# The head of a macaron block, written out in one order: setup, seven norms and five first FFNs

## The chip, the core and the metric

The kernel runs on one core of a Trainium2 chip. The metric is the device time of one execution in microseconds. Three runs of the kernel before took 2293.59, 2293.7 and 2294.9 us; their median is 2293.7.

A core has five engines that run side by side, each through its own list of instructions in order: TensorE (PE in the profile) multiplies matrices into PSUM, VectorE (DVE), ScalarE (ACT) and GpSimd (POOL) do elementwise work, and SyncE (SP) issues most of the transfers. An instruction that waits holds back all that stand behind it on its engine.

## The reference

The input is (4, 4096, 512) in float32, 128 row tiles of 128 rows. One block of a macaron transformer is computed:

```python
x = x + 0.5 * ffn(layernorm(x))
x = x + attention(layernorm(x))
x = x + 0.5 * ffn(layernorm(x))
```

`ffn` rounds its input and its 512x512 weight to a 6-bit grid in blocks of 32 (a scale from the largest magnitude of each block, then the nearest point of the grid), multiplies, and adds a bias; both calls share weight and bias. `attention` is neighbourhood attention with 16 heads of 32, in which each position sees 13 neighbours, with a table of relative position biases, a projection to Q, K and V and one out.

## The kernel before

**Data.** Each float32 operand of a product is split into two float16 parts, high and low. A product is three passes over four chunks, 12 matmuls of 128x128 by 128x512 (`product`, L139). The weights lie transposed and split in `wt`. A row tile's split operand is transposed by a DMA that SP issues (`low`, L195: DVE makes the low part, SP transposes both).

**One tile's way.** Load (`load`, L167), statistics, then the quantised norm (`quantised_norms`, L213): POOL makes the factors, ACT the normed tile `yq`, DVE the blocks' scales, POOL divides by them, ACT rounds to 8 bits, POOL scales back, ACT writes the high part of `hlq`, DVE the low, SP transposes into `xT`. Then the first FFN (`first_half`, L274): PE multiplies, DVE adds to x, statistics, POOL's factors, ACT, DVE, and a transpose into `x2`. Then V (`values`, L296). For each of the 128 items (a group of four tiles by a quarter of the heads) come Q and K (`project_qk`, L354: two products, ACT's high parts `qf` and `qk`, DVE's low parts, two spreading copies on ACT), scores (`ps`), softmax, attention (`attend`), the projection out, the last norm, the second FFN and the store.

**The order of the work.** The loop is a software pipeline written as slots: `begin(slot, stage, rank)` puts a stage into a slot, `run_slot` runs the stages of one slot by rank, and a stage is a generator whose `yield n, rank` puts its rest n slots further on. An item takes STEP = 7 slots. The first Q and K product stands in slot QK = 38.

**The head.** Everything ahead of slot 38 is the head (L673 to L891). Its first part, the setup, is left to a scheduler that orders instructions itself. It loads the FFN's weight `fw`, three biases on ACT's queue, three tiles of x and 16 chunks of the other weights (`rows`); takes the sums of squares of every weight chunk (ACT, 20 of them), from which `powers` makes the powers of two that put each weight on a good scale for float16; rounds the FFN's weight to the grid and scales it back with its power of two in `w_back` (L776, L780); splits it (L782, L783) and transposes it; and makes the norms of tiles 0 to 2. From L793 on the order is the program's own: the slots up to 37 run tiles 3 to 6 up to their norms, the first FFN of tiles 0 to 4, V of tiles 0 to 2, `put_scaled` (L795: ACT's high part and DVE's low part of one weight chunk, then its transpose) for the 16 chunks in slots 2 to 35, the attention bias `pmb` (L834, a product of its own) and the table of position biases (`put_table`).

**Buffers.** PSUM has three buffers for products (`ps_m`). The norms ahead of the loop share one `hlq`, one `q8` and two `yq`; split weights have four buffers (`whl`); `xT` has three. `qk`, `qf` and the loop's other tiles lie in memory that the setup's pools give back at L894.

Of the kernel before, what the change touches and what calls it, by code (L numbers as in the profile page):

```python
# [26 lines left out]
F32 = mybir.dt.float32  # L27
# [10 lines left out]
P = 128  # L38
HEADS = 16
# [24 lines left out]
def macaron_kernel(  # L64
# [148 lines left out]
    def quantised_norms(slot):  # L213
# [7 lines left out]
        if spare:  # L221
            y = xp.tile([P, dim], F32, tag="x", name=f"yq{slot}").unsqueeze(1)
        else:
            y = yp.tile([P, 2, dim], F32, tag="yq", bufs=2, name=f"yq{slot}")[:, :n]
# [16 lines left out]
        q8 = q8p.tile([P, 2, dim], F8, tag="q8", name=f"q8_{slot}")[:, :n]  # L241
# [6 lines left out]
        if spare:  # L248
            hl = xp.tile([P, dim], F32, tag="x", name=f"hlq{slot}").bitcast(F16)
            hl = hl.rearrange("p (u s k) -> p u s k", u=1, s=2)  # L250
        else:
            hl = hlp.tile([P, 2, 2, dim], F16, tag="hlq", name=f"hlq{slot}")[:, :n]
# [351 lines left out]
    EARLY = 3  # L604
# [35 lines left out]

    for t in range(NT):
        k = t * STEP
        sooner = (0, 2, 5, STEP)[t] if t <= EARLY else 0
        begin(k - 18 - (STEP if t == EARLY else 0), one(load, t), 0)
        slot = k - 10 - (10 if t == EARLY else 0)
        enlist(slot, t, "n1")
        if not 0 < t < EARLY:
            begin(slot - 1, one(moments, slot, t, "n1"), 1)
        begin(k + F1 - sooner, first_half(t))
        begin(k + V, values(t))  # L650
        begin(k + F1 - sooner, one(add_bias, t, half_ffn_b), 8)
# [6 lines left out]
    for slot in together:  # L658
        if together[slot][0][0][1] == "n3" or together[slot][0][0][0] >= EARLY:
            begin(slot, quantised_norms(slot), 1)  # L660
# [11 lines left out]

    with tc.tile_pool(name="setup", bufs=1) as sp, tc.tile_pool(name="scratch", bufs=2) as scr:  # L673
# [4 lines left out]
        rp = sp.tile([HEADS, NREL + 2 * (QR - 1)], F32, name="rp")  # L678
        for o in range(KC):
            nc.sync.dma_start(out=fw[:, o, :], in_=ffn_w[o * P : (o + 1) * P, :])  # L680
        nc.scalar.dma_start(out=half_ffn_b, in_=ffn_b.partition_broadcast(P))
        nc.scalar.dma_start(out=after_b, in_=proj_b.partition_broadcast(P))
        nc.scalar.dma_start(out=b12, in_=qkv_b.rearrange("(c p) -> c p", p=P))
        nc.gpsimd.memset(rp, 0.0)
        nc.scalar.dma_start(out=rp[:, QR - 1 : QR - 1 + NREL], in_=rpb)


        rows = {}

        sq = sp.tile([P, 5 * KC], F32, name="sq")  # L690
        first = min(slots)
        for slot in range(first, first + EARLY * STEP, STEP):
            run_slot(slot)
        for _ in quantised_norms(-10):
            pass
        chunks = (8, 9, 10, 11, 12, 13, 14, 15, 0, 4, 1, 5, 2, 6, 3, 7)
        for o in chunks:
            w, i = (qkv_w, o) if o < 3 * KC else (proj_w, o - 3 * KC)
            rows[o] = xp.tile([P, dim], F32, tag="x", name=f"rows{o}")
            nc.sync.dma_start(out=rows[o], in_=w[i * P : (i + 1) * P, :])  # L700
        for o in (*range(4 * KC, 5 * KC), *chunks):
            src = fw[:, o - 4 * KC, :] if o >= 4 * KC else rows[o]
            junk = scr.tile([P, dim], BF16, tag="junk", name=f"junk{o}")
            nc.scalar.activation(junk, src, AF.Square, accum_out=sq[:, o : o + 1])
        ptb = ps_m.tile([P, 512], F32, tag="mm", name="ptb")
        nc.tensor.transpose(ptb[:, : 3 * KC], b12, ident[: 3 * KC, : 3 * KC])
        bT = sp.tile([P, 3 * KC], F32, name="bT")
        nc.vector.tensor_copy(bT, ptb[:, : 3 * KC])
        b2 = sp.tile([P, 3 * KC], F32, name="b2")
        nc.vector.scalar_tensor_tensor(b2, bT, 2.0 ** -8, bT, ALU.mult, ALU.mult)  # L710
        nc.vector.tensor_tensor(sq[:, : 3 * KC], sq[:, : 3 * KC], b2, ALU.add)
        top5 = sp.tile([P, 5], F32, name="top5")
        up = sp.tile([P, 5], F32, name="up")
        down = sp.tile([P, 5], F32, name="down")

        def powers(lo, hi):

            w = hi - lo
            nc.vector.tensor_reduce(
                top5[:, lo:hi], sq[:, lo * KC : hi * KC].rearrange("p (m c) -> p m c", c=KC),  # L720
                AX.X, ALU.max,
            )
            ptn = ps_m.tile([P, 512], F32, tag="mm", name=f"ptn{lo}")
            nc.tensor.transpose(ptn[:w, :P], top5[:, lo:hi], ident)
            most = sp.tile([w, 1], F32, name=f"most{lo}")
            nc.vector.tensor_reduce(most, ptn[:w, :P], AX.X, ALU.max)
            diag = sp.tile([w, w], F32, name=f"diag{lo}")
            nc.vector.tensor_scalar(diag, ident[:w, :w], most, 2.0, ALU.mult, ALU.mult)
            ones_w = sp.tile([w, P], F32, name=f"ones{lo}")
            nc.gpsimd.memset(ones_w, 1.0)  # L730
            pb = ps_m.tile([P, 512], F32, tag="mm", name=f"pb{lo}")
            nc.tensor.matmul(pb[:, :w], ones_w, diag, start=True, stop=True)
            e = sp.tile([P, w], I32, name=f"e{lo}")
            nc.vector.tensor_copy(e.bitcast(F32), pb[:, :w])
            nc.vector.tensor_scalar(e, e, 23, None, ALU.logical_shift_right)
            nc.vector.tensor_scalar(e, e, 131, None, ALU.add)
            nc.vector.tensor_scalar(e, e, 1, None, ALU.logical_shift_right)
            nc.vector.tensor_scalar(e, e, 97, None, ALU.max)
            u, d = up[:, lo:hi].bitcast(I32), down[:, lo:hi].bitcast(I32)
            nc.vector.tensor_scalar(u, e, -1, 264, ALU.mult, ALU.add)  # L740
            nc.vector.tensor_scalar(u, u, 23, None, ALU.logical_shift_left)
            nc.vector.tensor_scalar(d, e, -10, None, ALU.add)
            nc.vector.tensor_scalar(d, d, 23, None, ALU.logical_shift_left)

        powers(4, 5)
        nc.vector.tensor_scalar(cf, down[:, 4:5], 0.5 / XS, None, ALU.mult)
        nc.gpsimd.tensor_scalar(half_ffn_b, half_ffn_b, 0.5, None, ALU.mult)

        def put_weights(o, hl):
            return nc.sync.dma_start_transpose(  # L750
                out=wt.rearrange("p s c o -> p (s c) o")[:, :, o * P : (o + 1) * P],
                in_=hl.rearrange("p s k -> p (s k)"),
            )

        w_sc, w_r, w_back = (
            sp.tile([P, KC * NB], F32, name=name) for name in ("w_sc", "w_r", "w_back")
        )
        for o in range(KC):  # L760
            nc.vector.tensor_reduce(
                w_sc[:, o * NB : (o + 1) * NB], blocks(fw[:, o, :]), AX.X, ALU.max,
                apply_absolute_value=True,
            )
        nc.vector.tensor_scalar(
            w_sc, w_sc, F8_SCALE / Q_MAX, F8_SCALE * Q_EPS, ALU.mult, ALU.max
        )
        nc.vector.reciprocal(w_r, w_sc)

        def per(t, o):  # L770
            return bc(t[:, o * NB : (o + 1) * NB], QB)

        for o in range(KC):
            fwb = blocks(fw[:, o, :])
            nc.vector.tensor_tensor(fwb, fwb, per(w_r, o), ALU.mult)
        nc.vector.tensor_scalar(w_back, w_sc, up[:, 4:5], None, ALU.mult)  # L776
        for o in range(KC):
            w8 = scr.tile([P, dim], F8, tag="w8_", bufs=KC, name=f"w8_{o}")
            nc.scalar.activation(w8, fw[:, o, :], AF.Identity, bias=w_nudge, saturate=False)
            nc.vector.tensor_tensor(blocks(fw[:, o, :]), blocks(w8), per(w_back, o), ALU.mult)  # L780
            hl = scr.tile([P, 2, dim], F16, tag="whl", bufs=4, name=f"whlf{o}")
            nc.scalar.copy(hl[:, 0, :], fw[:, o, :])  # L782
            nc.vector.tensor_tensor(hl[:, 1, :], fw[:, o, :], hl[:, 0, :], ALU.subtract)  # L783
            put_weights(4 * KC + o, hl)

        for t in range(1, EARLY):
            moments(t * STEP - 10, t, "n1")
            for _ in quantised_norms(t * STEP - 10):
                pass

        ctx.enter_context(tc.manual_schedule())  # L793

        def put_scaled(o):  # L795
# [6 lines left out]
            )  # L802
            put_weights(o, hl)

        su, sd = up, down
        tab = sp.tile([P, 1], F32, name="tab")
        vb = sp.tile([P, KC], F32, name="vb")

# [129 lines left out]
```

## Time and profile before

| | us |
|---|---|
| median of three runs | 2293.7 |
| the profiled execution, its own time | 2295.28 |
| its span, from first to last instruction | 2293.5 |
| first quantised tile's product pmf on PE | 37.04 |
| first Q and K product pmqk on PE | 82.39 |
| Q and K product of item 1 | 98.07 |
| Q and K product of item 2 | 109.21 |

Busy us of the engines, from the profile by stretch:

| stretch, us | PE | DVE | ACT | POOL | DMA share |
|---|---|---|---|---|---|
| 0 to 100 | 47.55 | 68.72 | 58.85 | 47.83 | 0.72 |
| 100 to 200 | 99.49 | 97.01 | 88.27 | 83.49 | 0.76 |
| 300 to 400 | 100.00 | 90.47 | 76.25 | 89.08 | 0.73 |
| 2000 to 2100 | 100.00 | 89.03 | 77.48 | 88.76 | 0.71 |
| 2100 to 2200 | 89.86 | 78.97 | 70.82 | 78.37 | 0.66 |

A row of the timeline gives the start, the time on the engine, the engine (SPq is SP's queue: the time that issuing takes), the line, the operation, what is written and from what, the count, and in brackets the idle time before it and what ended that. The chain of waits is the sequence of work that ended last, followed back from the last instruction. PE's granted clock is 1.00 at full speed.

### The profile page before, as it was taken

What the parts mean: (1) busy time and instruction counts of PE and PEld (TensorE: products, weight loads), DVE (VectorE), ACT (ScalarE), POOL (GpSimd) and SP (SyncE); (2) the same over time, 40 slices, a digit from 0 to 9 for tenths busy, and PEclk for the clock granted to TensorE, in tenths of its full rate; (3) what the DMA queues carried; (4) which work ended last, traced back from release to release, by engine and by line L of the source; (5) the groups of instructions that cost most, each with busy time, mean ns of one, the idle gap of its engine ahead of it and who ended that gap; (6) DMA issues with size and microseconds to landing.
All of it is one profiled execution on the core that took longest, in us unless ns stands there. A gap on an engine that the chain in (4) does not pass through costs nothing.

```text
span 2293.5 us, 65425 instructions
## 1 busy us (share of the span) xinstructions
PE 2214.2 (97%) x26771; PEld 1052.9 (46%) x26771; DVE 2011.7 (88%) x3769; ACT 1695.5 (74%) x2544; POOL 1969.2 (86%) x2006
## 2 busy tenths in 40 slices
PE   3799999999999999999999999999999999999978
PEld 1344444444444444444444444444444444444433
DVE  6899998888988988898988998888988988989775
ACT  5697777777777777777777777777777777777752
POOL 4588988988988988888888888888888889888776
PEclk9999999999999999999999999999999999999989
DMA  7687776777767777777776776777776777866654
GB/s 201 153 178 161 162 160 154 159 162 158 160 156 155 164 162 154 161 158 157 162 158 155 162 161 154 160 157 155 164 160 151 167 158 154 166 155 147 137 107 104
DMA packets 926213, 359.61 MB, mean 157 GB/s; under 512 B 719452, under 2 KB 890328, under 8 KB 925912
## 3 DMA queue, kind: packets, MB, share of 16 engines
q1 hardware_dynamic: 925568, 354.90, 70.8%
q8 instruction: 209, 3.42, 0.6%
q14 instruction: 92, 0.75, 0.1%
q10 hardware_dynamic: 344, 0.53, 0.1%
HBM read 110.26 MB, written 67.29 MB: 77 GB/s over the span
## 4 chain that ended last, share of the span: by engine, by line
PE 87%; DVE 7%; ACT 2%; POOL 2%; DMA 1%; issue 1%; SPq 0%; ACTq 0%; DVEq 0%; POOLq 0%
PE pmqk L144 27%; PE pmf L144 26%; PE pmo L144 14%; PE pmv L144 13%; PE ps L458 4%; PE pv L549 3%; DVE stn L173 1%; DVE hlq L197 1%; DVE hln L197 1%; DVE sc L232 1%; ACT qk L390 0%; DVE x L272 0%; POOL yq L239 0%; DVE total L514 0%; DVE qf L383 0%
## 5 line engine op out<-in xcount | busy, mean ns | idle before, releaser
L144 PE MATMUL pmf<-wt,xT 128*128 128x512 f16 x3048 | 702.7, 381 | 13.3 <-DMA xT<-hlq 7.4
L144 PE MATMUL pmqk<-x,wt 128*128 128x512 f16 x3072 | 705.8, 379 | 0.4 <-DVE after_b L836 0.4
L144 PEld LDWEIGHTS <-xT 128*128 128x128 f16 x3048 | 298.4, 98 | 377.2 <-DMA xT<-hlq 15.2
L144 PEld LDWEIGHTS <-wt 128*128 128x128 f16 x3072 | 289.7, 98 | 336.0 <-issue 1.3
L239 POOL TENSOR_TENSOR yq<-yq,r 128x1024 f32<-128x1024 f32 (+1 forms) x141 | 247.1, 1752 | 135.6 <-DVE r L237 124.1
L144 PE MATMUL pmv<-wt,x 128*128 128x512 f16 x1536 | 353.9, 380 | 4.2 <-DVE qf L383 2.6
L144 PE MATMUL pmo<-wt,ring 128*128 128x512 f16 x1536 | 357.2, 383 | 0.0
L390 ACT ACTIVATE qk<-qf,parity 128x1024 f16<-128x1024 f16 x256 | 349.3, 1432 | 0.0
L610 POOL TENSOR_TENSOR x<-x,half_ffn_b 128x512 f32<-128x512 f32 x256 | 327.8, 1281 | 0.0
L272 DVE SCALAR_TENSOR_TENSOR x<-pmf,coef,x 128x512 f32<-128x512 f32 x256 | 180.0, 703 | 144.7 <-PE pmf L144 141.1
L576 ACT ACTIVATE ring<-pv 128x510 f16<-128x510 f32 (+7 forms) x176 | 78.7, 475 | 307.3 <-PE pv L549 234.4
L173 DVE BATCH_NORM_STATS2 stn<-x 128x6 f32<-128x512 f32 x384 | 265.2, 691 | 8.8 <-DMA x<-in_L_attn_x_dram 0.2
L244 POOL TENSOR_TENSOR yq<-q,sc 128x1024 f32<-128x1024 fp8e4 (+1 forms) x141 | 246.2, 1746 | 4.8 <-ACT q L242 4.8
L144 PEld LDWEIGHTS <-x 128*128 128x128 f16 x1536 | 150.5, 98 | 186.9 <-issue 4.9
L242 ACT ACTIVATE q<-yq,nudge 128x1024 fp8e4<-128x1024 f32 (+1 forms) x141 | 150.0, 1064 | 115.9 <-POOL yq L239 107.6
L144 PEld LDWEIGHTS <-ring 128*128 128x128 f16 x1536 | 141.2, 98 | 160.5 <-issue 5.0
L518 POOL TENSOR_TENSOR sf<-sf,total 128x714 f32<-128x714 f32 (+2 forms) x128 | 178.7, 1396 | 37.2 <-DVE total L516 19.3
L226 ACT ACTIVATE yq<-x,nbq,rsq 128x512 f32<-128x512 f32 x254 | 193.1, 803 | 16.7 <-POOL nbq L185 15.2
L525 POOL TENSOR_TENSOR p<-sf,p 128x714 f16<-128x714 f32 (+2 forms) x128 | 192.5, 1504 | 0.0
L509 POOL TENSOR_TENSOR sf<-sf,top 128x714 f32<-128x714 f32 (+2 forms) x128 | 182.4, 1425 | 3.5 <-DVE top L507 3.3
L197 DVE TENSOR_TENSOR hlq<-yq,hlq 128x1024 f16<-128x1024 f32 (+1 forms) x141 | 167.6, 1189 | 8.7 <-ACT hlq L193 6.6
L610 POOL TENSOR_TENSOR x<-x,after_b 128x512 f32<-128x512 f32 x128 | 162.9, 1274 | 0.0
(143 smaller groups left out, 3441.0 us busy)
## 6 DMA issues: line engine op xcount, KB each, us to landing
vs<-vd SPq DMA_DIRECT2D x144, 357.0 KB
x<-in_L_attn_x_dram SPq DMA_DIRECT2D x128, 256.0 KB
vd<-vt SPq DMA_DIRECT2D x128, 256.0 KB
out_dram<-x SPq DMA_DIRECT2D x128, 256.0 KB
vs<-vd SPq DMA_DIRECT2D x24, 378.0 KB
vs<-vd SPq DMA_DIRECT2D x24, 315.0 KB
rows<-in_L_attn_qkv_w_dram SPq DMA_DIRECT2D x12, 256.0 KB
xT<-hlq SPq DMA_TRANSPOSE x141
```

The source lines that it names most:

```text
L144: nc.tensor.matmul(pm, lhs(a, c), rhs(b, c), start=(n == 0), stop=(n == 3 * KC - 1))
L173: nc.vector.bn_stats(st, xs[t])
L197: nc.vector.tensor_tensor(hl[:, :, 1, :], y, hl[:, :, 0, :], ALU.subtract)
L226: nc.scalar.activation(y[:, u], xs[t], AF.Identity, bias=nb[:, u : u + 1], scale=rs[:, u : u + 1])
L239: nc.gpsimd.tensor_tensor(yb, yb, bc(r, QB), ALU.mult)
L244: nc.gpsimd.tensor_tensor(yb, q8.rearrange("p u (n q) -> p (u n) q", q=QB), bc(sc, QB), ALU.mult)
L272: nc.vector.scalar_tensor_tensor(xs[t], pm, cf, xs[t], ALU.mult, ALU.add)
L390: nc.scalar.activation(to, whole[0], AF.Copy, scale=parity[:, e : e + 1])
L509: nc.gpsimd.tensor_tensor(s, s, bc(top[:, :n], KN), ALU.subtract)
L518: nc.gpsimd.tensor_tensor(s, s, bc(total[:, :n], KN), ALU.mult)
L525: nc.gpsimd.tensor_tensor(p[:, :n, KN : 2 * KN], s, ph, ALU.subtract)
L610: nc.gpsimd.tensor_tensor(xs[t], xs[t], b, ALU.add)
```

## The change

The whole head becomes one list of pieces, each with a number, and is issued by the program in the order of these numbers (`at`, `spread_out`, L878 to L964 of the changed kernel); nothing of it is left to the scheduler, and no slot below 38 is used. The numbers run from 0.7 to 69.0; they set the order and nothing else. In detail:

- The list holds the setup, the norms of tiles 0 to 6 to their end, the first FFN of tiles 0 to 4 to its end and V of tiles 0 and 1. V of tile 2 goes into slot 39, and the product `pmb` of the attention bias into slot 47, behind item 1's Q and K product.
- The seven norms get buffers of their own for `yq`, `q8` and `hlq`, one tile each, in the setup's pool. `xT` still has three buffers.
- The FFN's weight is scaled back without its power of two (`per(w_sc, o)`, `w_back` is gone); the power is applied when it is split, by the same `split` that splits the other chunks.
- The biases `half_ffn_b` and `after_b` and the table `rpb` are loaded on SP's queue behind 27 loads; only the QKV bias is left on ACT's.
- The other 16 weight chunks are split after the first FFN of tile 1, four buffers as before.
- Two dozens of matmuls whose result nobody reads stand on PE behind the first and the last split of the FFN's weight.

```diff
-    def quantised_norms(slot):
+    def quantised_norms(slot, own=None):
...
-        if spare:
+        if own:
+            y = own.tile([P, 1, dim], F32, name=f"yq{slot}")
+        elif spare:
...
-        nc.vector.tensor_scalar(w_back, w_sc, up[:, 4:5], None, ALU.mult)
...
-            nc.vector.tensor_tensor(blocks(fw[:, o, :]), blocks(w8), per(w_back, o), ALU.mult)
-            hl = scr.tile([P, 2, dim], F16, tag="whl", bufs=4, name=f"whlf{o}")
-            nc.scalar.copy(hl[:, 0, :], fw[:, o, :])
-            nc.vector.tensor_tensor(hl[:, 1, :], fw[:, o, :], hl[:, 0, :], ALU.subtract)
...
+        def scaled_back(o):
+            nc.vector.tensor_tensor(blocks(fw[:, o, :]), blocks(w8[o]), per(w_sc, o), ALU.mult)
+
+        def split(o):
+            s = up[:, o // KC : o // KC + 1]
+            hl = scr.tile([P, 2, dim], F16, tag="whl", bufs=4, name=f"whl{o}")
+            nc.scalar.activation(hl[:, 0, :], rows[o], AF.Copy, scale=s)
+            yield
+            nc.vector.scalar_tensor_tensor(
+                hl[:, 1, :], rows[o], s, hl[:, 0, :], ALU.mult, ALU.subtract
+            )
+            nc.sync.dma_start_transpose(
...
+            if o in (4 * KC, 5 * KC - 1):
+                idle = ps_s.tile([P, 512], F32, tag="s", name=f"idle{o}")
+                for _ in range(12):
+                    nc.tensor.matmul(idle, hl[:, 1, :P], hl[:, 1, :], start=True, stop=True)
...
-        begin(0, one(scales), 9)
-        for slot, o in zip((2, 4, 5, 6, 10, 13, 16, 19, 21, 23, 25, 27, 29, 31, 33, 35), chunks):
-            begin(slot, put_scaled(o), 9)
-        begin(20, attention_bias(), 9)
-        begin(26, one(put_table), 9)
...
+        for o, key in enumerate((0.7, 1.1, 1.6, 2.0)):
+            at(key, load_ffn, o)
+        for t, key in enumerate((2.4, 2.9, 5.0, 5.4, 7.6, 11.4, 11.9, 57.0, 64.0)):
+            at(key, load, t)
...
+        at(12.3, lambda: nc.sync.dma_start(out=half_ffn_b, in_=ffn_b.partition_broadcast(P)))
+        at(12.7, lambda: nc.sync.dma_start(out=after_b, in_=proj_b.partition_broadcast(P)))
+        at(13.2, lambda: nc.sync.dma_start(out=rp[:, QR - 1 : QR - 1 + NREL], in_=rpb))
+        at(14.9, lambda: nc.gpsimd.tensor_scalar(half_ffn_b, half_ffn_b, 0.5, None, ALU.mult))
+        for h in range(4):
+            at(13.6 + 0.5 * h, put_masks, h)
+        at(15.8, put_shifts)
+        for i, key in enumerate((16.6, 17.2, 24.3, 24.9, 25.5, 26.1, 26.7, 27.3)):
+            at(key, put_shifted, i // 4 * 2, i % 4)
...
+        for o, h, l in zip(
+            (8, 9, 10, 11, 0, 4, 1, 5, 2, 6, 3, 7, 12, 13, 14, 15),
+            (40.2, 40.9, 41.6, 42.3, 43.1, 44.4, 45.9, 46.7, 48.8, 49.5, 50.3, 51.0, 54.6, 55.3, 56.6, 57.4),
+            (41.9, 42.6, 44.1, 45.7, 46.5, 47.2, 51.0, 51.7, 52.5, 53.2, 53.9, 56.0, 58.6, 60.1, 61.7, 62.5),
+        ):
+            spread_out(split(o), h, l)
...
+        NORMS = (
+            (6.3, 7.3, 9.1, 11.7, 12.9, 15.9, 17.4, 18.9, 20.1),
+            (14.9, 16.2, 20.2, 21.5, 22.8, 24.3, 25.1, 26.7, 27.4),
+            (22.7, 23.9, 25.8, 28.1, 29.9, 31.4, 33.5, 35.0, 36.7),
...
+            (26.5, 42.7, 51.7, 63.9, 65.1, 66.3, 67.1, 68.3, 69.0),
+        )
+        for t, keys in enumerate(NORMS):
+            slot = t - 1000
+            enlist(slot, t, "n1")
+            at(keys[0], moments, slot, t, "n1")
+            spread_out(quantised_norms(slot, sp), *keys[1:])
+        FIRST = (
+            (26.0, 29.3, 31.2, 32.3, 33.6, 35.1),
+            (31.2, 33.9, 35.8, 36.8, 38.1, 40.5),
...
+        for t, (keys, bias) in enumerate(zip(FIRST, (15.0, 21.1, 27.4, 31.0, 40.2))):
+            spread_out(first_half(t), *keys)
+            at(bias, add_bias, t, half_ffn_b)
...
+        for _, _, f, args in sorted(order, key=lambda e: e[:2]):
+            f(*args)
...
+    begin(QK + 1, values(2), 6)
+    begin(QK + 9, bias_product(), 9)
+    slot = QK
```

## The prediction

> **What bounds the kernel now.** I read the page first: PE is busy 97% of the span, and the row of 40 slices puts nearly all that is missing into the first two slices. Then busy time by stretch, cut where item 1's Q and K product starts (98.07, from the PE timeline) and at 2100.
>
> ```profile
> PE 2214.2 (97%) x26771; PEld 1052.9 (46%) x26771; DVE 2011.7 (88%) x3769; ACT 1695.5 (74%) x2544; POOL 1969.2 (86%) x2006
> ```
> ```profile
> 98.07:2100.00 2001.93, 1999.98 (x24557) 955.90 (x24550) 1804.82 (x3349) 1533.63 (x2276) 1778.18 (x1766) 1.00 0.73 159
> ```
> From 98.07 to 2100 PE is idle for 1.95 us (column two less column three). Whatever the head saves or loses moves everything behind it by as much. So the question is when item 1's pmqk starts in the changed kernel, and which PE work stands ahead of it. The PE timeline around it:
>
> ```profile
> 82.39 5.50 PE L144 MATMUL pmqk<-x,wt 128*128 128x512 f16 x24 [0.43 <-DVE after_b L836]
> 87.73 2.75 PE L144 MATMUL pmf<-wt,xT 128*128 128x512 f16 x12
> 93.10 4.21 PE L144 MATMUL pmv<-wt,x 128*128 128x512 f16 x12 [2.62 <-DVE qf L383]
> 97.24 0.90 PE L458 MATMUL ps<-qk 64*64 64x84 f16 x64
> 98.07 5.35 PE L144 MATMUL pmqk<-x,wt 128*128 128x512 f16 x24
> ```
> Last comes the chain of waits. It ends the head on ACT's first qf (91.58), held by a weight transpose: the qf tile lies in memory that the setup gives back. Two more views price the changed head: SP's issues, and what the DMA engines moved in each us from 0 to 40.
>
> ```profile
> 88.34 3.05 DMA wt<-whl
> 91.58 0.69 ACT qf L379
> ```
> ```profile
> 24.50 4.11 SPq L750 DMA_TRANSPOSE wt<-whlf  x3
> ...
> 31.44 2.71 SPq L847 DMA_DIRECT2D shifted<-rd  x4
> ...
> 78.19 2.69 SPq L750 DMA_TRANSPOSE wt<-whl  x2
> ```
> ```profile
> GB/s 0 53 154 195 227 384 400 380 291 293 264 313 387 391 408 408 397 391 391 387 385 358 143 3 0 45 204 192 180 182 254 134 142 51 32 160 128 53 37 104
> ```
> So SP needs 1.35 us for a transpose and 0.65 for a shifted copy, and the loads run at about 390 GB/s, 0.67 us for each 256 KB.
>
> **What ends the changed head.** In the changed kernel's order of instructions qf of item 0 waits for the transpose of norm 6, the last DMA of the head; its own tiles lie where qf goes. I call the landing of that transpose Tq (91.58 in before) and the start of item 1's pmqk T1 (98.07). The PE work ahead of T1 is as before, less pmb, whose 12 matmuls (2.6 us) now come behind it. So the change costs T1 - 98.07 + 2.6.
>
> **Step 1, the loads.** In the code a DMA on SP waits until the eighth before it has landed. Before, x0 stood still till 5.78 for half_ffn_b, and its 26 loads (6.8 MB) were in at about 22.4. Now half_ffn_b is the 28th load: two more are 1.3 us, and the dip in slices 8 to 11 (0.4 MB short of 390, 1.0 us) may fill. I take 22.5; the ends are 20.5 (28 at 0.67 from 1.7) and 23.7. The written order wants it at 14.9, and POOL, which runs in order, has the half of it (1.51) and x0's bias (1.27) ahead of norm 1's factors (three small ones, 1.2 with gaps) and of norm 0's scaling back (1.1): done at 27.6. ACT's high part (0.62) and DVE's low part (0.68) follow: 29.0. Before, that low part began at 26.21.
>
> **Step 2, the first two FFNs.** SP stands at rd until rp has landed, just behind the biases (23.0), then issues rd (0.69), one weight transpose (25.1), waits for rd (unseen; as a transpose's 2.8 us, 26.4), two shifted copies (27.7), two weights (30.4), norm 0 (31.7), the last FFN weight, which lands at 31.7 + 2.8 = 34.5. pmf_0 begins there, 2.5 us ahead of before (37.04). Six shifted copies (3.9) stand ahead of norm 1's transpose: issued 37.0, landed 39.8, pmf_1 done at 42.5. Its x (0.72), three DVE pieces ahead in the queue (0.28, 0.22 and a low part at 0.6 from start to start), statistics (0.85), factors (1.4, as from 59.23 to 60.64), yn and its high part (1.33) and the low part (0.69) end at 48.6.
>
> **Step 3, SP from there.** Behind it SP has 24 transposes (16 of them weights) and 4 copies (0.55 each): 24 x 1.35 + 2.2 = 34.6 us. Never waiting, the last is issued at 48.6 + 34.6 - 1.35 = 81.9 and lands at 84.7. It will wait. The 16 weights share four buffers; from the fifth on, ACT's split (0.72) needs a landed transpose, so a chunk takes (0.72 + 0.75 + 1.35 + landing) / 4: 1.41 at 2.8 us, 1.7 if landing grows to 4 in a full queue (a load already took 5: issued 7.89, used 12.84). That is up to 4.2 over twelve chunks. Norm 6 ends in a chain of POOL, ACT, POOL, ACT, DVE (1.05, 0.72, 1.04, 0.61, 0.68 = 4.1) that two transposes (2.7) don't cover: up to 1.4. So Tq is 84.7 to 90.3; no row is nearer to either end, and I take the middle, 87.5. With the loads at their ends it would be 85.5 or 88.7.
>
> **Step 4, from Tq to T1.** Three PSUM buffers are held by pmqk's two and pmv_2, so pmf_5 waits for qf's low part: 0.69 + 0.75. In before it had run ahead (87.73). PE has then stood for some 8 us. After 2.62 us of standing pmv took 4.21 instead of 2.75, after 4.54 pmf took 4.45, after 1.54 pmv took 2.76. So: 1.5 + 4.45 + pmv 2.6 + ps 0.83 = 9.4, against 6.5 in before. T1 = 96.9.
>
> **Sum.** 96.9 - 98.07 + 2.6 = +1.4. The profiled execution took 2295.28 (span 2293.5), 1.6 above the median of the three runs; against the median the forecast is 2293.7 + 1.4 = **2295.1**.
>
> **Edits at nothing.** Own hlq buffers take away ACT's two waits for a landed transpose (1.35 and 1.71), but POOL's late half_ffn_b is now what hlq waits for. The power of two at the split takes away w_back (0.82) and lengthens four copies by 0.11 and four DVE low parts by about 0.1: nothing, as DVE stands before low part 0 anyway. The 24 idle matmuls (0.44 each cold, 10.6) lie where PE stood 22.9 us; they cost only if the second dozen, from about 29.7, runs past 34.5 (5.3 cold: by 0.5). The masks stand at POOL's start in the trace of before too (2.03 to 3.66). Seven norms done ahead shorten no part of the loop: there PE sets the pace, and after_b's 0.75 on DVE falls under a DVE of 90%.
>
> Of the idle dozens the Trainium skill says, in "TensorE: Matmul & The Clock Gate", section "What's actually happening", that the array falls to half rate after an idle window of about 3.4 us. The trace shows it slow after 2.62 already. By the rule or by the row the dozens may keep pmf_0 warm (2.75 for 5.30), which is 2.5 us on x0, but pmf_1 waits for norm 1's transpose (39.8) either way, and pmf_5 is cold: the sum is the same.
>
> **Rivals.**
> *Faster: the written order nearly holds.* half_ffn_b lands by 18 (it isn't issued before the 20th load is in, 1.7 + 20 x 0.67 = 15.1, and takes a lone transpose's 2.8), and SP then starts its run five to seven us earlier, until DVE is the limit: from x0's update to the end its queue is 35 us of work. For it: the dip of slices 8 to 11 and the slow first five us may both go. Against it: loads came at the full rate, with 5 us from issue to use. Tq = 80, T1 = 89.4, 2287.6. Chance 0.17.
> *Slower: the four weight buffers set the pace.* ACT runs in order; while a split waits for a landed transpose, yn and the high parts of the first FFNs stand behind it, and SP behind those, which delays the landing of the next. It decides once issue to landing passes 2.6 us (1.35 x 4 less 0.72, 0.75 and 1.35), and the rows have 2.8 to 3.05 with an unloaded queue. At 4.4 a chunk takes 1.8, twelve of them 5.4 over SP's pace, on top of 87.5: Tq = 92.9, T1 = 102.3, 2300.5; POOL and DVE in each other's way (whl's low part 0.88 in the mean, 0.74 at its shortest, sixteen times) makes it 2302.7. Against it: before has this loop too, and there DVE, not ACT, was late for most chunks (2.3 us of waiting for ACT's split in sixteen). Chance 0.33.
> *About the same: SP sets the pace, as summed.* Own range 2289 to 2299. Chance 0.50.
>
> **The numbers.** The range reaches half way into both rivals: 2286.5 to 2303. A difference of 0.2%, 4.6 us, is about what a measurement here tells from none. Faster 0.17, within it 0.50, slower 0.33.
>
> **What would show it.** Right: half_ffn_b's half on POOL at 21 to 24; pmf_0 near 34.5; SP's transposes back to back from about 48; qf waiting for norm 6's transpose at about 87.5; pmf_5 at 4.2 us or more. Wrong: half_ffn_b by 18, or ACT rather than SP waiting longest between 48 and 85, or a loop in which PE stands for more than 2 us between T1 and 2100.

## The result and the profile after

The changed kernel takes **2305.28 us** (median of five runs, 2304.0 to 2306.06) against 2293.7 of the kernel before in the same comparison (2293.19 to 2295.01): ratio 1.0050, 95% interval 1.0038 to 1.0061, 11.6 us slower. Its profiled execution took 2305.28 (span 2303.3), 10.0 more than that of before. The forecast was 2295.1, the range ended at 2303.

The shares in the page's busy row are as they were within one per cent, since PE sets the pace of the whole (its 24 further matmuls are the idle ones). The stretch behind the start of item 1's pmqk (T1, now 107.18), from the view by stretch (columns as before), is as full as it was too:

```profile
PE 2223.0 (97%) x26795; PEld 1054.9 (46%) x26795; DVE 2015.3 (87%) x3770; ACT 1695.9 (74%) x2544; POOL 1968.4 (85%) x2006
```
```profile
107.18:2100.00 1992.82, 1990.85 (x24450) 950.56 (x24443) 1796.08 (x3330) 1522.71 (x2263) 1767.95 (x1755) 1.00 0.74 159
```
From T1 to 2100 PE is idle for 1.97 us (1992.82 less 1990.85; 1.95 before). So the loss lies in the head. PE's timeline of it:

```profile
36.92 2.75 PE L144 MATMUL pmf<-wt,xT-1000_358 128*128 128x512 f16 x12 [1.33 <-issue]
41.88 4.45 PE L144 MATMUL pmf<-wt,xT-999_453 128*128 128x512 f16 x12 [2.21 <-DMA xT-999_453<-hlq-999_448]
...
82.17 7.48 PE L144 MATMUL pmqk<-x,wt 128*128 128x512 f16 x24 [8.77 <-DVE r-995_772 L239]
...
98.95 5.04 PE L144 MATMUL pmf<-wt,xT-995_804 128*128 128x512 f16 x12 [6.70 <-DVE qf L390]
...
107.18 1.04 PE L144 MATMUL pmqk<-x,wt 128*128 128x512 f16 x4
```
The first tile's FFN begins where it did (36.92; 37.04 before), item 0's pmqk too (82.17; 82.39), and T1 is 9.1 us later. The chain of waits of the head tells what was late:

```profile
18.29 4.79 DMA after_b<-in_L_attn_proj_b_dram
23.13 1.51 POOL half_ffn_b L901
...
39.08 2.76 DMA xT-999_453<-hlq-999_448
...
57.42 3.27 DMA wt<-whl
...
61.57 3.22 DMA wt<-whl
...
71.39 3.23 DMA wt<-whl
...
80.70 3.09 DMA wt<-whl
...
94.27 3.04 DMA xT-994_828<-hlq-994_826
```
The names: xT-1000 to xT-994 are the transposed norms 0 to 6. The chain passes through the late biases, through norm 1's transpose, four times through the landing of a weight transpose, and ends on norm 6's. ACT's waits, up to 110 us (total, times, longest):

```profile
ACT whl L808 <- DMA wt<-whl: 15.4, 6, 5.7
ACT hlq-1000_352 L193 <- POOL yq-1000_249 L249: 8.8, 1, 8.8
...
ACT qf L386 <- DMA xT-994_828<-hlq-994_826: 4.3, 1, 4.3
```
Line one is ACT standing at a split until a weight buffer is free again; line two is norm 0 behind the late half_ffn_b; line three is qf, which the prediction let wait for norm 6. In the kernel before no split waited so: its 16 other weights begin at 42.62 and take 47 us, here they begin at 57.42 and go through the same four buffers in 31.

### The profile page after: what moved, and what is told of

It reads as the page before. It is cut to its first block, busy times and chain, and to the rows that moved or that the text cites. A ratio compares the mean times of both kernels' runs of the same rounds, so it can differ in the third digit from the quotient of the medians.

```text
span 2303.3 us, 65461 instructions
## 1 busy us (share of the span) xinstructions
PE 2223.0 (97%) x26795; PEld 1054.9 (46%) x26795; DVE 2015.3 (87%) x3770; ACT 1695.9 (74%) x2544; POOL 1968.4 (85%) x2006
## 4 chain that ended last, share of the span: by engine, by line
PE 89%; DVE 5%; DMA 2%; ACT 2%; POOL 1%; issue 1%; SPq 0%; ACTq 0%; POOLq 0%; DVEq 0%
PE pmqk L144 27%; PE pmf L144 27%; PE pmo L144 14%; PE pmv L144 13%; PE ps L465 4%; PE pv L556 3%; DVE stn L173 1%; DMA wt<-whl 1%; DVE hlq L197 0%; DVE hln L197 0%; ACT qk L397 0%; DVE sc L234 0%; POOL yq L241 0%; POOL yq L249 0%; DVE x L279 0%
## 5 line engine op out<-in xcount | busy, mean ns | idle before, releaser
L144 PE MATMUL pmf<-wt,xT 128*128 128x512 f16 x2988 | 686.4, 380 | 6.9 <-DMA xT<-hlq 5.5
L144 PEld LDWEIGHTS <-xT 128*128 128x128 f16 x2988 | 291.7, 98 | 361.9 <-DMA xT<-hlq 7.7
L241 POOL TENSOR_TENSOR yq<-yq,r 128x1024 f32<-128x1024 f32 (+1 forms) x136 | 241.3, 1774 | 121.1 <-DVE r L239 108.3
L249 POOL TENSOR_TENSOR yq<-q,sc 128x1024 f32<-128x1024 fp8e4 (+1 forms) x136 | 240.9, 1772 | 1.9 <-ACT q L247 1.9
```

The lines of the kernel that those rows point to most:

```text
L144: nc.tensor.matmul(pm, lhs(a, c), rhs(b, c), start=(n == 0), stop=(n == 3 * KC - 1))
L241: nc.gpsimd.tensor_tensor(yb, yb, bc(r, QB), ALU.mult)
L249: nc.gpsimd.tensor_tensor(yb, q8.rearrange("p u (n q) -> p (u n) q", q=QB), bc(sc, QB), ALU.mult)
```

## The experiments

**Theory A:** two costs one behind the other, POOL's 8.2 us of waiting for half_ffn_b and, later, the four weight buffers. **Rivals:** the late bias alone (B), SP's 1.35 us a transpose (C), POOL's chain of the last norms (D). The first three runs also test whether the parts add up; a fourth takes up the order in which memory comes free. T1 below is that of the profiled execution; "against before" is the median less that of before in the same comparison.

| run | T1 | against before, us | ratio, 95% |
|---|---|---|---|
| after | 107.18 | +11.6 | 1.0038 to 1.0061 |
| e1, bias first | 108.62 | +14.7 | 1.0047 to 1.0077 |
| e2, six weight buffers | 103.52 | +8.7 | 1.0022 to 1.0050 |
| e3, e1 and e2 | 105.19 | +12.2 | 1.0034 to 1.0064 |
| e5, norms 5 and 6 in the loop's tiles | 101.97 | +7.5 | 1.0020 to 1.0043 |
| e6, copies late | 108.82 | +14.4 | 1.0047 to 1.0074 |
| e7, e1 and e6 | 106.89 | +11.8 | 1.0035 to 1.0062 |
| e8, e2, e5 and e7 | 98.08 | +4.4 | 1.0010 to 1.0028 |
| e9, no pmb | 107.16 | +10.7 | 1.0027 to 1.0055 |
| e10, e1 and the copies in SP's gap | 102.87 | +7.3 | 1.0020 to 1.0044 |
| e11, e2, e5 and e10 | 94.72 | -0.5 | 0.9990 to 1.0008 |
| e12, e11 and pmb in the head | 95.56 | -2.0 | 0.9983 to 1.0001 |
| e13, before with the power at the split | 97.00 | -0.9 | 0.9987 to 1.0005 |
| e15, e2 and e5 | 98.68 | +4.9 | 1.0011 to 1.0030 |
| e4, no idle matmuls | 107.02 | +10.1 | 1.0029 to 1.0062 |

### The bias, the buffers, the release of memory

e1:
```diff
-        at(12.3, lambda: nc.sync.dma_start(out=half_ffn_b, ...
+        at(0.8, lambda: nc.scalar.dma_start(out=half_ffn_b, ...
```


> Edit: half_ffn_b is loaded on ACT's queue beside b12, at the very start, in place of the 28th load on SP's; nothing else. T1 is the start of item 1's Q and K product (107.18 after, 98.07 before), and behind it nothing should change, so the time should follow T1 one for one. Theory A (two costs: POOL stands 8.2 us for half_ffn_b at about 23, and later the four weight buffers set the pace): the half runs before 12 us, norm 0's low part ends near 22 in place of 28.95, the run of weight transposes begins 3 to 6 us sooner, and the buffers still hold it: T1 102 to 104, 2300 to 2302. Rival B (the late bias is the whole loss): T1 at or under 98, 2295 or less. Rival C (the four buffers, or SP, set the pace from 48 on whatever comes before): T1 within 1.5 of 107.2, 2304 to 2306.

Norm 0's low part came 4.5 us sooner (24.44 for 28.95), and nothing followed: PE stood 9.2 us for a weight transpose, and pmf_0 began later than in the kernel after.

```profile
38.09 5.01 PE L144 MATMUL pmf<-wt,xT-1000_358 128*128 128x512 f16 x12 [9.23 <-DMA wt<-whl]
```
T1 is 108.62. B falls, and so does that half of A: a wait of eight us on three engines gave nothing back when it was taken away. The edit has prices of its own, though. SP's loads waited 2.2 us for half_ffn_b, rd left 0.67 us later (24.71), and pmf_0 ran slower (5.01 for 2.75; below, "cold" and "warm"). What lay beside the wait is in SP's timeline of the kernel after:

```profile
24.04 0.65 SPq L850 DMA_DIRECT2D rd<-rp  x1
...
28.24 1.27 SPq L854 DMA_DIRECT2D shifted<-rd  x2
29.61 2.65 SPq L813 DMA_TRANSPOSE wt<-whl  x2
...
35.04 3.93 SPq L854 DMA_DIRECT2D shifted<-rd  x6
39.08 1.26 SPq L198 DMA_TRANSPOSE xT-999_453<-hlq-999_448  x1
```
rd waits for the last load, the first shifted copy waits for rd to land (28.24), the FFN's weights stand behind it, and six more copies stand ahead of norm 1's transpose, whose low part began at 36.00 and took 0.69.

e2:
```diff
-            hl = scr.tile([P, 2, dim], F16, tag="whl", bufs=4, name=f"whl{o}")
+            hl = scr.tile([P, 2, dim], F16, tag="whl", bufs=6, name=f"whl{o}")
```


> Edit: six buffers for the split weights in place of four; nothing else. ACT waits 15.4 us for landed weight transposes in the kernel after. Theory A (the buffers set the pace): these waits fall under 4 us, norm 6's transpose is issued 5 to 9 us sooner (94.27 after), T1 98 to 102, 2296 to 2300. Rival C (SP's 1.35 us a transpose sets the pace, and ACT's waits are only its image): ACT's waits shrink but T1 moves by less than 1.5, 2304 to 2306. Rival D (POOL's chain of the last norms sets it): the weights end sooner, but norm 6's transpose is issued within 2 us of 94.27, T1 105 or later, 2303 or more.

```profile
ACT whl L808 <- DMA wt<-whl: 8.2, 7, 3.3
```
```profile
90.23 1.24 SPq L198 DMA_TRANSPOSE xT-994_828<-hlq-994_826  x1
```
ACT's waits for landed weights fell from 15.4 to 8.2, norm 6's transpose was issued at 90.23 (94.27), T1 103.52. The gain is under the forecast of A, but T1 moved by 3.7 where C allowed 1.5, so C falls; and D, which had norm 6 hardly moved, falls too. The buffers are a real part of the loss, though A had made too much of them.

> Edit: both of the above, half_ffn_b at the start on ACT's queue and six weight buffers. Theory A: the two add up, as they act on two stretches one behind the other: T1 94 to 98, 2291 to 2296. If they are one cost seen twice: T1 no lower than the better of the two alone, by 1.5. With SP as the pace behind 48 (rival C): T1 as in the kernel with the bias first alone.

The two edits together: T1 105.19, worse than the buffers alone by about what the bias edit costs alone (1.7 and 1.4). That is also the sign that was set for one cost seen twice, but a cost seen twice would have shown a gain in e1 too. So the early part of A was wrong and the late part stands.

e5:
```diff
-            spread_out(quantised_norms(slot, sp), *keys[1:])
+            spread_out(quantised_norms(slot, sp if t < 5 else None), *keys[1:])
```


> Edit: the last two of the seven norms take the loop's tiles in place of own ones in the setup's pool; nothing else. Then the setup's memory is free without norm 6's transpose having landed, and qf of item 0 should wait for the table's last operation (92.93 to 93.6) in place of the landing at 97.31. Theory A (a part of the loss sits in the order of release, apart from pace and bias): qf near 93.6, pmf_5 some 3.7 us sooner, T1 103 to 104, 2301 to 2302. Rival (norm 6's high part now waits for norm 5's landed transpose and eats the gain): T1 106 to 108, 2304 to 2306.

As expected by A, and more: ACT's timeline has qf at 93.91, behind DVE's last operation on the setup's tiles, no longer behind a transfer.

```profile
93.91 0.69 ACT L386 ACTIVATE qf<-pmqk,qk_b 128x512 f16<-128x512 f32 x1 [0.54 <-DVE vbx L876]
```
pmf_5 then began at 95.92 (98.95) and ran warm, 2.75 for 5.04, so T1 is 101.97: 5.2 us, of which 2.3 is PE's clock. That part can't be counted on: in e11 the same product stood as long (3.06 us; 3.08 here) and ran cold, 4.40. qf needs nothing of norm 6. It waited only because norm 6's own tile lay in the pool whose memory qf's pool takes over.

### The copies in SP's order

**Theory E:** SP's order holds the first FFNs (rd, the copies), and POOL's late bias counts only once that is mended. e6 moves the nine issues; e7 is e6 with e1.
```diff
-        at(15.8, put_shifts)
-        for i, key in enumerate((16.6, 17.2, 24.3, 24.9, 25.5, 26.1, 26.7, 27.3)):
+        at(36.0, put_shifts)
+        for i, key in enumerate((36.8, 36.9, 37.0, 37.1, 37.2, 37.3, 37.4, 37.5)):
```


> Edit: the copy rd<-rp and the eight copies shifted<-rd are issued on SP behind norm 2's transpose and ahead of norm 3's, in place of among the FFN's weights and ahead of norm 1's transpose; nothing else. New theory E (what the run with the bias first taught: POOL's 8.2 us wait was cover, not cost; SP's order holds the first two FFNs, as rd waits there for rp, the first shifted copy for rd, and six more stand ahead of norm 1's transpose): norm 1's transpose follows its low part (36.0 to 36.7) in place of 39.08, pmf_1 begins near 39.6 (41.88), and all behind it moves up as much: T1 104 to 105.5 (107.18), 2302 to 2303.5. With half_ffn_b still late, no more than 3 us can come. Rival F (the late bias and SP each cover the other, so neither alone gives anything): T1 within 1 of 107.2, 2304.5 to 2306.

> Edit: the copies late as in the run beside this one, and half_ffn_b first on ACT's queue; nothing else. Theory E: with both gone pmf_0 begins at 30 to 33 (36.92) and pmf_1 at 35 to 37 (41.88): T1 100 to 102.5, 2298 to 2301. So the bias, which alone gave nothing (T1 108.62), would be worth some 3 us more once SP is out of the way. Rival F': the loads themselves (FFN weights, then x) or DVE's queue hold pmf_1 at 39 or later: T1 no lower than with the copies late alone.

Half right. pmf_1 began at 39.78 in e6 (expected 39.6) and at 36.93 in e7 (35 to 37), from 41.88. But T1 was 108.82 and 106.89: the gain was given back at once. SP in e7:

```profile
50.26 5.15 SPq L854 DMA_DIRECT2D shifted<-rd  x8
...
56.88 1.25 SPq L198 DMA_TRANSPOSE xT-997_600<-hlq-997_578  x1
58.23 2.67 SPq L813 DMA_TRANSPOSE wt<-whl  x2
```
Norm 3's low part began at 51.31, its transpose was issued 4.9 us behind the low part's end, and the first of the other weights (58.23; 57.42 in the kernel after) behind that. The copies cost what they delay, wherever they stand. In e7 SP stood from 33.4 (xT-999's issue) to 44.86; e10 puts them there, right behind norm 1's transpose, with the bias first:
```diff
-        at(15.8, put_shifts)
-        for i, key in enumerate((16.6, 17.2, 24.3, 24.9, 25.5, 26.1, 26.7, 27.3)):
+        at(27.6, put_shifts)
+        for i, key in enumerate((28.0, 28.2, 28.4, 28.6, 28.8, 29.0, 29.2, 29.4)):
```


> Edit: half_ffn_b first on ACT's queue, and rd with the eight shifted copies issued on SP right behind norm 1's transpose (SP stood there from 33.4 to 46.9 in the run with the copies late and the bias first); nothing else. Theory E, place by place: the nine issues cost what they delay. Among the FFN's weights they held pmf_0 and pmf_1, ahead of norm 3's transpose they held that and the first weight (56.88 and 58.23, with the low part ready at 51.3). In the gap they should delay nothing: norm 3's transpose near 52.7, first weight transpose 53.5 to 55, T1 102 to 104 (106.89), 2299.5 to 2302. Rival: the gap is no gap, as rd's wait or the copies' queue holds norm 2's transpose past 48: T1 106 or later, 2304 or more.

```profile
33.30 0.65 SPq L850 DMA_DIRECT2D rd<-rp  x1
37.31 5.16 SPq L854 DMA_DIRECT2D shifted<-rd  x8
...
52.73 1.26 SPq L198 DMA_TRANSPOSE xT-997_600<-hlq-997_578  x1
54.08 6.80 SPq L813 DMA_TRANSPOSE wt<-whl  x5
```
It all came as written: norm 3's transpose 52.73, first weight 54.08, T1 102.87, +7.3 us, 2301.2. SP's 3.3 us of waiting for rd are still there, and now they hold nobody. The pair of edits is worth 4.3 us of T1. No run has the copies there with the bias still late, so how the 4.3 divides is not shown.

### Both stretches, pmb, and the parts costed at nothing

> Edit: copies late, bias first, six weight buffers, the last two norms in the loop's tiles; the other parts of the change stay. Theory E with A: the gains act one behind the other (first FFNs 5 to 6 us, buffers 3.7, release 5.2 of which some 3 remain once the buffers are six): T1 92 to 96 against 98.07 before; pmb's 2.6 us still lie behind it: 2288 to 2294, so at last equal to the kernel before (2293.3) or a little faster. If SP or DVE is the next bound (rival): T1 97 to 100, 2293 to 2298.

T1 98.08 and 2297.9 are the rival's numbers, and SP it was: the copies were still in the wrong place (first weight 56.74). The T1 of before, met by chance, tells something of pmb: at the same T1 the span is 2295.8 against 2293.5, 2.3 more. One pair is too little for a price, though. From T1 to the end of the span the twelve profiled kernels with pmb behind T1 take 2195.4 to 2198.6 us, the three with it ahead (before, e12, e13) 2194.6 to 2195.4: 1.7 more on average, with a spread of 3.2.

> Edit: the four repairs of the earlier run (bias first, copies moved, six weight buffers, two norms in the loop's tiles) with the copies in SP's gap. Theory E: another 3 to 4.5 us off T1 (98.08): 93.5 to 95. Whether the time follows is open since the run without pmb, where 2.6 us saved behind T1 came back as a wait for the V stack at 182: if PE alone sets the pace behind T1, 2293 to 2295.5; if DVE's and SP's chain to the first attend sets it, within 1.5 of the 2297.9 of that run.

T1 94.72, 2293.34: the loss is gone. Together with e15, the late pair alone, the parts add up:

> Edit, on the kernel after: only the two late repairs (six weight buffers, the last two norms in the loop's tiles); the copies and half_ffn_b stay where the change put them. If the loss is two stretches one behind the other (theory E with A): T1 is that of the run with all four in their best place plus what the early two gave there (107.18 - 102.87 = 4.3): 94.7 + 4.3 = 99.0, and the time 2297 to 2299.5. If the repairs are not additive (the late ones only work once the early ones have made room): T1 no better than the 101.97 of the norms alone, 2300 or more.

T1 98.68 (99.0 expected), 2298.8. The early pair takes 4.3 from T1 (e10), the late pair 8.5 (e15), all four 12.5 (e11), 12.8 if they simply added. Two things make this fit better than it is. PE's clock differs in ways that nearly cancel: pmf_0 ran warm in e11 (2.75) and cold in e10 (5.28), pmf_5 cold in e11 (4.40) and warm in e15 (2.75). And e15's profiled execution, 2296.02, is the fastest of its ten. By the medians the early pair takes 4.3, the late pair 6.7 and all four 12.1.

pmb was taken out (e9: its stage is not begun, and the kernel leaves out what the bias of V adds to the output), and put ahead of pmf_5 (e12):
```diff
-        pmb = ps_m.tile([P, dim], F32, tag="mm", name="pmb")
+        pmb = ps_v.tile([P, dim], F32, tag="v", name="pmb")
...
-    begin(QK + 9, bias_product(), 9)
+    begin(QK + 1, bias_product(), 7)
```


> Edit: the kernel after without the 12 matmuls of pmb and the one DVE operation that adds them to after_b; it leaves out what the bias of V adds to the output. Prices the term +2.6 of the sum, which the change moved from the head, where PE stood, into the loop, where PE sets the pace. If the term is real: T1 as after (107.2), time 2.0 to 3.2 below after's 2305.3: 2302 to 2303.3. If the loop's other engines hide it: within 1 of 2305.3.

> Edit: as the run beside this one, and pmb's 12 matmuls put ahead of pmf_5, in a PSUM bank that no one uses yet, where PE waits for qf. If the term +2.6 of the sum is real there: 1 to 2.6 us below the run beside this one. If the chain to the first attend hides it (as the run without pmb suggests: 1.1): within 1.2 of it.

e9 is 1.1 us under after's 2305.28 with intervals that overlap; its span is the same 2303.3, with T1 at 107.16. PE in e9:

```profile
182.48 0.71 PE L556 MATMUL pv<-pT,vs 126*32 126x30 f16 x68 [2.63 <-DMA vs<-vd]
```
In the kernel after this product begins at 182.69 without a wait. The 2.6 us that PE saved it stood for a V stack to land, 5.66 us of that run's chain of waits. So in this run pmb lay beside a transfer, and the term was hidden. e12 is 1.4 us under e11 although its T1 is 0.84 later, but their intervals overlap. The term is worth something between 0 and the 2.3 of e8; what decides is not shown beyond e9's one transfer. e12 is the best version found: 2291.91 against 2293.86, but its interval (0.9983 to 1.0001) still holds no change.

e13, on the kernel before (w_back goes, the split takes the scalar):
```diff
-        nc.vector.tensor_scalar(w_back, w_sc, up[:, 4:5], None, ALU.mult)
...
-            nc.vector.tensor_tensor(blocks(fw[:, o, :]), blocks(w8), per(w_back, o), ALU.mult)
-            nc.scalar.copy(hl[:, 0, :], fw[:, o, :])
+            nc.vector.tensor_tensor(blocks(fw[:, o, :]), blocks(w8), per(w_sc, o), ALU.mult)
+            nc.scalar.activation(hl[:, 0, :], fw[:, o, :], AF.Copy, scale=up[:, 4:5])
...
```


> Edit, on the kernel before: the power of two is applied where the FFN's weight is split (ACT's copy with a scale, DVE's low part with the same scalar), and w_back goes; this part of the change alone. The prediction costs it at nothing. If so: T1 within 1.5 of 98.07 and the time within 2 of 2293.5. If the longer copies count, or the scheduler places the four scalings so that norm 0 comes later: T1 99.5 to 102, 2295 to 2298.

2293.0, within the interval no change; T1 97.00. That part costs nothing.

e4:
```diff
-            if o in (4 * KC, 5 * KC - 1):
+            if o in ():
```


> Edit, on the kernel after: the two dozens of idle matmuls are left out (their results are read by no one). The prediction put them at nothing, pmf_0 warm or not. pmf_0 ran warm in the kernel after (2.75) and pmf_1, behind 2.2 us of standing, cold (4.45). Without the dozens pmf_0 should run cold (4.4 to 5.3) from 36.9 and pmf_1 follow it at once, warm, at about 42: x0 comes 2 us later and x1 1 to 1.5 us sooner. As DVE and POOL take them in order, x0 first, the later x0 decides: T1 107.5 to 109, 2305.5 to 2307.5. If x1 decides (rival): T1 105.5 to 107, 2303 to 2305.

As expected pmf_0 ran cold (4.87) and pmf_1 warm behind it (2.76). T1 (107.02) lies between the two guesses: norm 3's transpose came 1.35 us later than in the kernel after, and nothing of that was left at T1. The median, 2303.92, is the one forecast for x1 deciding, and within the intervals it is no change. The dozens only move a cold run from one tile to the next.

## Why the prediction was wrong

**What bounds it, and the sum: right in form.** Cost = T1 - 98.07 + 2.6 gives 11.7 with the measured T1; the medians differ by 11.6, the profiled runs by 10.0. That the medians agree so well is partly luck, as the 2.6 is the soft term: 2.3 between e8 and before, none in e9's profiled run.

Of the 10.2 us between forecast and result, 6.1 arose in step 2, 3.4 in the waiting of step 3, 0.2 in norm 6's landing (3.04 for 2.8) and 0.5 in step 4.

**Step 1, the loads: right, and of no weight by itself.** half_ffn_b's half began at 23.13 (22.5 was taken, 20.5 and 23.7 the ends), norm 0's low part ended at 29.64 (29.0). In e1, taking this wait away alone gave nothing.

**Step 2, the first two FFNs: the first failed step.** It put the end of tile 1's low part at 48.6; it came at 54.71. Of these 6.1 us, 2.1 are pmf_1's start (41.88 for 39.8: rd was issued at 24.04 for 23.0, the first copy 4.2 us behind it for 3.4, and all that follows on SP moved along). Another 1.8 are a cold pmf_1 (4.45 for 2.7). PE had stood 2.21 us; in the step's own sum it stands some 2.5, close to the 2.62 after which its row has 4.21, and the product was taken as warm all the same. The last 2.2 are the path from its end to the low part (46.37 to 54.71 for 6.1 us): DVE takes the other weights' powers and scales, 49.47 to 54.1, ahead of it. ACT's high part was done at 52.10, and DVE came to the low part at 54.03. Two of these small operations met POOL (0.93 and 0.90 us where their like take 0.17), so an estimated 1.5 of the 2.2 us comes from that:

```profile
50.56 1.04 POOL L249 TENSOR_TENSOR yq-997_462<-q_-997_540,sc-997_475 128x512 f32<-128x512 fp8e4 x1
50.70 0.93 DVE L766 TENSOR_SCALAR up<-up 128x4 int32<-128x4 int32 x1
```
The step counted three DVE pieces ahead of x1's low part and missed the powers, for which all 16 weights wait too.

**Step 3, SP from there: the second failed step.** SP never waiting would have taken 33.3 us from the low part's end to norm 6's issue; 2.8 of waiting were added, 5.6 as the end, and it took 39.5 (54.74 to 94.27), 6.2 of waiting. Tq was 97.31 for 87.5. What held SP was ACT standing for landed weights, 15.4 us, as the slower rival said; with six buffers SP's waiting fell to 2.1 (e2, 54.81 to 90.23). The rival had the mechanism and, by adding on to step 2's 48.6, still a T1 of 102.3: even its dearest sum, 2302.7, lacks the late step 2. And the mechanism is worth less alone (e2: 3.7) than with the release (e15: 8.5).

**The own buffers, costed at nothing: wrong.** The prediction saw that qf would wait for norm 6, and took that for given. It is the price of putting norms 5 and 6 into the setup's pool: 5.2 us (e5), 3.0 of them pmf_5's start and the rest its clock.

**Step 4, Tq to T1: right.** 9.9 us measured, 9.4 forecast; pmf_5 5.04 cold (4.45).

**The other edits at nothing: right** within the intervals, for the power of two (e13) and the idle matmuls (e4).

So the loss is two stretches. In the first, up to norm 3's transpose, mending SP's order and the late bias takes 4.3 us off T1. In the second, mending the four buffers and the release of the setup's memory takes 8.5. With both mended the written order is ahead of before at T1 by 3.35 us (94.72), but not in time beyond the interval: pmb stands behind T1.

**Open:** what of the first stretch is POOL and DVE in each other's way was not tried by itself. e1's median lies 2.8 us over after's where T1 is 1.4 later, but its profiled execution, 2305.75, is the lowest of its four, and the intervals overlap.

## What to carry to other kernels

In an order written by hand, price an instruction by who stands behind it on its queue, not by its own time. A transfer that waits for another's landing belongs where its queue is idle anyway. A long wait in a profile may only lie beside other waits: undo it and see whether the end moves before believing it. And a tile in a pool that will be given back can make the next pool's first user wait for the tile's last reader (4.3 us of ACT here), so try the last work of a phase with its tiles elsewhere. When two runs are compared by a start time such as T1, see first whether PE's products ahead of it ran warm in both.

## What the runs showed of the hardware

**When PE slows down.** The product of tile 3, after different idle times: 1.74 us (e1), 1.82 (e9), 1.86 (e12) and 1.88 (e4) of standing left 2.76; 2.23 (e15), 2.31 (after) and 2.43 (e11) made it 4.27 to 4.45. From e4 and e15, PE's timeline, the idle time in the brackets:

```profile
60.74 2.76 PE L144 MATMUL pmf<-wt,xT-997_574 128*128 128x512 f16 x12 [1.88 <-DMA xT-997_574<-hlq-997_552]
```
```profile
59.72 4.45 PE L144 MATMUL pmf<-wt,xT-997_600 128*128 128x512 f16 x12 [2.23 <-DMA xT-997_600<-hlq-997_578]
```
So about two us of standing can be enough (pmf_1 in e9 took 4.19 after 2.01). But the idle time alone does not decide. The product pmf_5, from e5 and from e11:

```profile
95.92 2.75 PE L144 MATMUL pmf<-wt,xT-995_804 128*128 128x512 f16 x12 [3.08 <-DVE qf L390]
```
```profile
87.09 4.40 PE L144 MATMUL pmf<-wt,xT-995_804 128*128 128x512 f16 x12 [3.06 <-DVE qf L390]
```
It was warm after 2.04 (e8) and 2.69 (e15) too, and V's two products took 5.34 after 2.92 (e1) and 8.25 after 2.95 (e3). What else decides is not shown here. In "TensorE: Matmul & The Clock Gate", section "What's actually happening", the Trainium skill gives about 3.4 us for the idle window; the cold products after 2.01 to 2.43 us do not agree with that as the least standing that slows PE, and the rows decide.

**DVE and POOL in each other's way.** A scaling of 4 by 4 numbers takes DVE 0.22 us in the kernel after (47.34), where POOL stands. In e8 it meets two POOL operations and lasts until the second is over:

```profile
40.59 1.04 POOL L241 TENSOR_TENSOR yq-997_453<-yq-997_453,r-997_469 128x512 f32<-128x512 f32 x1
40.72 1.94 DVE L754 TENSOR_SCALAR diag<-ident,most 4x4 f32<-4x4 f32 x1
41.59 1.04 POOL L241 TENSOR_TENSOR yq-996_471<-yq-996_471,r-996_498 128x512 f32<-128x512 f32 x1
```
DVE ends at 42.66, POOL's second at 42.63. The Trainium skill says in "Trainium Architecture — The Big Picture", section "What this means for kernel authors", that the two share a pair of ports under an exclusive lock; this row agrees, for this operation. In e1 and e11 the same row took 1.93 us: DVE loses 1.7 us here in each of these earlier heads. What T1 loses by it was not tried.
